# V by Strassen products kept in DRAM, q scaled during K's projection, and the softmax moved by one turn, in an attention and mixture-of-experts block

## The chip, the core and the metric

The kernel runs on one core of a Trainium2 chip, with all data in fp32. The time is what one execution takes on the device, in microseconds (us); the median of several executions is given. A profile is one execution recorded by the hardware. In it PE is TensorE's matmuls, PEld its weight loads, DVE VectorE, ACT ScalarE, POOL GpSimd, and SP the engine that issues the DMAs. An fp32 matmul leaves two records on PE.

## The reference, cut to what matters

```python
# x: (2, 512, 512); Wq, Wk, Wv: (512, 4096); Wo: (4096, 512); 32 heads of 128
h = layernorm(x)
q, k, v = h @ Wq + bq, h @ Wk + bk, h @ Wv + bv
q, k = rms_norm(q, gq), rms_norm(k, gk)             # over all 4096 columns
attn = softmax(einsum('bhqd,bhkd->bhqk', q, k) / sqrt(128))
x = x + layernorm(einsum('bhqk,bhkd->bhqd', attn, v) @ Wo + bo)
f = layernorm(x)
x = x + layernorm(f @ W_base.T + b_base + moe(f))   # 8 experts of rank 16, gated
```

## The kernel before

There are two batches of 512 tokens, 32 heads of 128 columns, and eight groups of four heads (a group is 512 columns of a weight). Heads and batches together make N = 64 pairs (head, batch), and the main loop goes over these 64 turns, head by head, both batches of a head one after the other.

**Norm and transposition.** `norm_transposed` (L132) normalizes the four token tiles of a batch and transposes them on PE. `xTs` holds the result for both batches: four tiles of 128 x 512 each, with the columns of `h` on the partitions.

**Projections of q and k.** `project` (L173) computes them transposed, one group of four heads at a time, by a Strassen scheme with seven products for eight blocks. The blocks are the two halves of the contraction, the two batches, and the two halves of a group's columns. `token_sums` (L150) makes the sums of tokens once. `weight_sums` (L162) makes the four sums of weights of each group on POOL, for the next group while PE works on this one. Each of the seven products is made for two head columns `j`, with two matmuls each (L192), and leaves PSUM by a DVE addition (L223 to L251) or, for the first, by an ACT activation that also adds the bias (L219). So a group has 28 matmuls on PE and 14 DVE operations. A finished head is stored in DRAM (`keptq`, `keptk`, L206), squared on ACT (L212) and added up on POOL (L213) for the RMS norm. Its tiles come from a pool of five buffers, `qpool` for q and `kpool` for k.

**Scales.** After K's first group the reciprocal root of q's mean square is made for all tokens (`rqs`, L284 to L286). After all of K, `key_scales` (L288) makes that of k.

**The head loop** (L434 to L455) does all else of the attention. One turn `i` issues:

- `fetch(i + 3)` (L315): loads k and q of that pair from DRAM; `scaled(i + 2)` (L323): multiplies q by its norm and by gq times gk, on DVE
- `sums(i)` (L345): three DVE additions over the four key tiles of the exponentials
- `scores(i + 1)` (L329): four matmuls (`pss`, L335), each leaving PSUM by ACT with k's scale (L336), then three DVE maxima (L338 to L340) and an all-reduce over the partitions on POOL (L342)
- `outward` (L398): products of an earlier group's outputs with Wo (`psy`, L404), dealt by the table `o_tasks`
- `values` (L304): V of a coming group, four matmuls for each token tile (`psv`, L308), leaving PSUM by an ACT copy (L310), dealt by `v_tasks`; V stays in SBUF, in 16 buffers
- `turned(i)` (L354): a DVE transposition and a reduction; `exponentials(i + 1)` (L374): a DVE subtraction of the maximum over 128 x 2048 (L376) and the exponential on ACT (L377)
- the additions of `outward` on DVE (L405)
- `weighted(i)` (L381): four matmuls of exponentials and V (`o`, L386); `reciprocals(i)` (L362): a small matmul (`psd`, L365), a reciprocal and a transposition on DVE; `divided(i)` (L389): a multiplication on DVE and the bias on ACT

**What sets the order.** PE, DVE, ACT and POOL run their instructions in the order of the code (`manual_schedule`, L575). SP's order is set by the framework: a DMA is queued when a planner holds its buffer and its data to be ready, and SP then takes its queue in order. PSUM has eight banks in two tags of four, `ps` and `aux`; `pt` (L68) takes them in turn if no tag is named.

**After the loop** the last group's outward products, the residual, a second norm and the mixture of experts (`ffn`, L501) follow.

Of the kernel before, what the change touches and what calls it, by code (L numbers as in the profile page):

```python
# [10 lines left out]
F32 = mybir.dt.float32  # L11
AF = mybir.ActivationFunctionType
ALU = mybir.AluOpType
# [18 lines left out]
def kernel(ctx: ExitStack, tc: tile.TileContext, x, wq, wk, wv, wo, vecs, rows, wbase, gates, bexp, out):  # L32
# [8 lines left out]

    nc = tc.nc
# [6 lines left out]
    vpool = ctx.enter_context(tc.tile_pool(name="vpool", bufs=2 * B * NT))  # L49
    qpool = ctx.enter_context(tc.tile_pool(name="qpool", bufs=5))  # L50
    kpool = ctx.enter_context(tc.tile_pool(name="kpool", bufs=5))
    opool = ctx.enter_context(tc.tile_pool(name="opool", bufs=GH * B + 10))
    spool = ctx.enter_context(tc.tile_pool(name="spool", bufs=3))
    tmp = ctx.enter_context(tc.tile_pool(name="tmp", bufs=6))
    wpool = ctx.enter_context(tc.tile_pool(name="wpool", bufs=4))
# [48 lines left out]
    gate_sb = const.tile([P, NK, E * R + E + 1], F32, tag="gate", name="gate_sb")  # L104
    nc.sync.dma_start(out=gate_sb, in_=gates.rearrange("(c p) f -> p c f", p=P))
    bexp_sb = const.tile([P, D], F32, tag="bexp", name="bexp_sb")
    nc.sync.dma_start(out=bexp_sb, in_=bexp)
# [42 lines left out]
    def token_sums(xTs):  # L150

        (b11, b21), (b12, b22) = ((xT[0:2], xT[2:4]) for xT in xTs)
        first, second = wide("t12"), wide("t34")
        t1, t2, t3, t4 = first[:, 0:2], first[:, 2:4], second[:, 0:2], second[:, 2:4]
        for c in range(2):
            nc.vector.tensor_tensor(t1[:, c], b12[c], b11[c], ALU.subtract)
            nc.vector.tensor_tensor(t2[:, c], b22[c], t1[:, c], ALU.subtract)  # L157
            nc.vector.tensor_tensor(t3[:, c], b22[c], b12[c], ALU.subtract)
            nc.vector.tensor_tensor(t4[:, c], b21[c], t2[:, c], ALU.subtract)
        return [[t[:, c] for c in range(2)] for t in (t1, t2, t3, t4)]  # L160
# [12 lines left out]
    def project(xTs, sums, w_src, bias, step, name, pool, keep, accs, w):  # L173
# [8 lines left out]
        parts = weight_sums(w, f"{name}0")  # L182
        for g in range(G):
# [20 lines left out]
            def keep_it(o, b, j):  # L204
                h = g * GH + j
                nc.sync.dma_start(out=keep[b, h], in_=o)  # L206
# [3 lines left out]
                else:  # L210
                    sq = tt(f"sq_{name}{b}_{h}")
                    nc.scalar.activation(sq, o, AF.Square)  # L212
                    nc.gpsimd.tensor_tensor(accs[b], accs[b], sq, ALU.add)  # L213

# [13 lines left out]
            t1, t2, t3, t4 = sums  # L228
            u2 = [tile_of("u2", j) for j in two]
            for j in two:  # L230
                ps = product(6, s2, t2, j)
                nc.vector.tensor_tensor(u2[j], ps, u1[j], ALU.add)
            u3 = [tile_of("u3", j) for j in two]
            for j in two:
                ps = product(7, s3, t3, j)
                nc.vector.scalar_tensor_tensor(u3[j], ps, column(step, j), u2[j], ALU.add, ALU.add)
            for j in two:
# [3 lines left out]
                keep_it(o, 0, j + 2)  # L241
            for j in two:
# [4 lines left out]
                keep_it(o, 1, j + 2)  # L247
            for j in two:
# [6 lines left out]
    def attention():  # L255
# [9 lines left out]
        rqs = [const.tile([P, 512], F32, tag=f"rq{b}", name=f"rq{b}") for b in range(B)]  # L265
# [3 lines left out]
        accq = [xpool.tile([P, 512], F32, tag="x", name=f"accq{b}") for b in range(B)]  # L269
        acck = [xpool.tile([P, 512], F32, tag="x", name=f"acck{b}") for b in range(B)]  # L270

        steps = const.tile([P, 2, H], F32, tag="steps", name="steps")
        for i in range(2):
            of, to = (v.rearrange("p (g j) -> p g j", j=GH) for v in (vec[:, i, :], steps[:, i, :]))
            nc.vector.tensor_tensor(to[:, :, 0:2], of[:, :, 2:4], of[:, :, 0:2], ALU.subtract)
        sums4 = []
        for _ in project(xTs, sums4, wq, bq, steps[:, 0, :], "q", qpool, keptq, accq, wq0):
            pass
        wk0 = load_w(wk[:, ts(0, GH * P)], "w_k0")
        for g in project(xTs, sums4, wk, bk, steps[:, 1, :], "k", kpool, keptk, acck, wk0):  # L280
            if g == 0:
                for b in range(B):
# [3 lines left out]
                    nc.vector.reciprocal(rqs[b], rqs[b])  # L286

# [7 lines left out]
        vs, wvs, wos = {}, {}, {}  # L295

        def load_wv(g):
            if g < H // GH:
# [314 lines left out]
```

## Time and profile before

| what | value |
|---|---|
| median of 3 runs | 1385.29 us (1385.04 to 1387.31) |
| the profiled execution | 1385.63 us, of which its span (first to last instruction) is 1383.9 |
| granted TensorE clock, mean | 0.991 |
| busy DVE, ACT, POOL | 907.3, 503.7, 351.0 us |
| DMA, whole span | 109.84 MB, mean 79 GB/s |
| stages in the span | start to 37 us; q to 224; k to 418; head loop to 1287; rest to 1384 |
| issue to landing, 256 KB: store of q, of k; load of q, of k | 2.5, 2.4; 2.9, 2.6 us (medians) |

A row of the profile by lines gives line, engine, operation, tiles out<-in, shapes and count, then busy time and the mean of one in ns, and the idle time before with what ended it. A row of the timeline gives start, duration, and the same names. In a table of windows each row is a stretch of time with the busy time of each engine and its instructions in brackets, then the granted clock, the busy share of the 16 DMA engines, and GB/s.

### The profile page before, as it was taken

How to read it: one execution, taken by the hardware profiler on the slowest of the kernel's cores; microseconds unless marked ns; L12 is line 12 of the kernel's file. 1: busy time of each engine (PE TensorE's matmuls, PEld its weight loads, DVE VectorE, ACT ScalarE, POOL GpSimd, SP SyncE). 2: the span in 40 equal slices, each digit the busy share in tenths (PEclk: the TensorE clock that was granted, in tenths of full speed). 3: DMA queues.
4: the chain of work that ended last, by engine and by line, in shares of the span. 5: the costliest groups of instructions: out<-in, count | busy, mean ns of one | idle time of the engine just before them, and what ended most of it. 6: DMA issues, size and time to landing. Idle time of an engine off the chain costs nothing.

```text
span 1383.9 us, 10495 instructions
## 1 busy us (share of the span) xinstructions
PE 1342.4 (97%) x3308; PEld 610.3 (44%) x3308; DVE 907.3 (66%) x1350; ACT 503.7 (36%) x703; POOL 351.0 (25%) x262
## 2 busy tenths in 40 slices
PE   4999999999999999999999999999999999999976
PEld 2444444444444444444444444444444444444443
DVE  6443434534343888778778777777777777887556
ACT  4122222322224444344434344343434343443333
POOL 3357556565731111111111111111111111111000
PEclk9999999999999999999999999999999999999998
DMA  6243344434333112103112111211111111200001
GB/s 231 91 150 124 117 149 144 161 106 152 122 118 118 61 46 76 46 31 107 40 37 76 61 46 61 67 40 64 58 61 42 65 48 59 76 23 16 23 1 61
DMA packets 58759, 109.84 MB, mean 79 GB/s; under 512 B 5072, under 2 KB 5712, under 8 KB 58704
## 3 DMA queue, kind: packets, MB, share of 16 engines
q1 hardware_dynamic: 58704, 109.17, 23.2%
q8 instruction: 26, 0.43, 0.1%
q14 instruction: 29, 0.24, 0.1%
HBM read 73.50 MB, written 35.65 MB: 79 GB/s over the span
## 4 chain that ended last, share of the span: by engine, by line
PE 95%; DVE 3%; ACT 1%; issue 1%; POOL 0%; DVEq 0%; POOLq 0%; ACTq 0%
PE pss L335 16%; PE psy L404 16%; PE o L386 16%; PE psv L308 15%; PE p_k L192 14%; PE p_q L192 14%; PE f L517 2%; PE f L567 1%; PE psd L365 1%; PE hg L509 1%; DVE same L264 0%; PE nt_f L139 0%; PE nt_a L139 0%; DVE nT_a L144 0%; ACT n_a L137 0%
## 5 line engine op out<-in xcount | busy, mean ns | idle before, releaser
L342 POOL PARTITION_ALL_REDUCE top<-m x64 | 114.1, 1783 | 738.7 <-DVE m L340 738.7
L335 PE MATMUL pss<-qh,kh 128*128 128x512 f32 x512 | 235.2, 602 | 0.0
L386 PE MATMUL o<-s,v 128*128 128x512 f32 x512 | 230.2, 592 | 0.0
L308 PE MATMUL psv<-wv,nT_a 128*128 128x512 f32 x512 | 229.5, 592 | 0.0
L404 PE MATMUL psy<-wo,oh 128*128 128x512 f32 x512 | 228.2, 592 | 0.0
L376 DVE TENSOR_TENSOR s<-s,top 128x2048 f32<-128x2048 f32 x64 | 146.7, 2292 | 42.5 <-POOL top L342 42.5
L377 ACT ACTIVATE s<-s 128x2048 f32<-128x2048 f32 x64 | 122.2, 1910 | 89.4 <-DVE s L376 88.4
L336 ACT ACTIVATE s<-pss,rk 128x512 f32<-128x512 f32 x256 | 154.0, 680 | 0.8 <-PE pss L335 0.8
L386 PEld LDWEIGHTS o<-s,v 128*128 128x128 f32 x512 | 97.3, 190 | 122.5 <-issue 122.2
L308 PEld LDWEIGHTS psv<-wv,nT_a 128*128 128x128 f32 x512 | 97.1, 190 | 121.5 <-issue 121.0
L404 PEld LDWEIGHTS psy<-wo,oh 128*128 128x128 f32 x512 | 97.1, 190 | 121.5 <-issue 121.0
L310 ACT COPY v<-psv 128x512 f32<-128x512 f32 x64 | 37.4, 586 | 275.8 <-PE psv L308 275.8
L335 PEld LDWEIGHTS pss<-qh,kh 128*128 128x128 f32 x512 | 92.5, 190 | 92.8 <-issue 92.8
L213 POOL TENSOR_TENSOR accq<-accq,sq_q 128x512 f32<-128x512 f32 x62 | 78.6, 1268 | 95.0 <-ACT sq_q L212 94.5
L393 ACT ACTIVATE oh<-oh,vec 128x512 f32<-128x512 f32 x64 | 46.0, 719 | 144.0 <-DVE oh L392 144.0
L213 POOL TENSOR_TENSOR acck<-acck,sq_k 128x512 f32<-128x512 f32 x62 | 78.6, 1267 | 75.4 <-ACT sq_k L212 75.0
L367 DVE RECIPROCAL inv<-psd 128x16 f32<-128x16 f32 x64 | 16.4, 256 | 118.4 <-PE psd L365 118.4
L192 PE MATMUL p_q<-t,s_q 128*128 128x512 f32 x192 | 88.0, 608 | 3.6 <-DVE t L157 3.6
L212 ACT ACTIVATE sq_q<-q 128x512 f32<-128x512 f32 x62 | 39.1, 630 | 134.3 <-DVE q L240 79.2
L212 ACT ACTIVATE sq_k<-k 128x512 f32<-128x512 f32 x62 | 39.1, 631 | 127.9 <-DVE k L240 71.4
L192 PE MATMUL p_k<-t,s_k 128*128 128x512 f32 x192 | 85.0, 592 | 0.0
L192 PEld LDWEIGHTS p_q<-t,s_q 128*128 128x128 f32 x192 | 37.3, 195 | 51.3 <-issue 48.8
(146 smaller groups left out, 1440.2 us busy)
## 6 DMA issues: line engine op xcount, KB each, us to landing
keptq<-q SPq DMA_DIRECT2D x64, 256.0 KB, 2.5
qh<-keptq SPq DMA_DIRECT2D x64, 256.0 KB, 2.9
keptk<-k SPq DMA_DIRECT2D x64, 256.0 KB, 2.4
kh<-keptk SPq DMA_DIRECT2D x64, 256.0 KB, 2.6
w_q<-in_wq SPq DMA_DIRECT2D x8, 1024.0 KB, 6.9
w_k<-in_wk SPq DMA_DIRECT2D x8, 1024.0 KB, 5.6
wv<-in_wv SPq DMA_DIRECT2D x8, 1024.0 KB, 5.6
wo<-in_wo SPq DMA_DIRECT2D x8, 1024.0 KB, 5.0
```

What stands on the lines that cost most here:

```text
L192: nc.tensor.matmul(ps, a[:, c, ts(j, P)], x[c], start=(c == 0), stop=(c == 1))
L212: nc.scalar.activation(sq, o, AF.Square)
L213: nc.gpsimd.tensor_tensor(accs[b], accs[b], sq, ALU.add)
L308: nc.tensor.matmul(ps, xTs[b][c][:, ts(t, P)], wvs[g][:, c, :], start=(c == 0), stop=(c == NK - 1))
L335: nc.tensor.matmul(ps, kk[i][:, ts(k, P)], qs[i], start=True, stop=True)
L336: nc.scalar.activation(s[:, k, :], ps, AF.Copy, scale=rks[b][:, k : k + 1])
L342: nc.gpsimd.partition_all_reduce(top, m, P, ReduceOp.max)
L376: nc.vector.tensor_tensor(s, s, top.unsqueeze(1).to_broadcast([P, NT, 512]), ALU.subtract)
L377: nc.scalar.activation(s, s, AF.Exp)
L386: nc.tensor.matmul(po, vs[b, g, k][:, ts(j, P)], ss[i][:, k, :], start=(k == 0), stop=(k == NT - 1))
L393: nc.scalar.activation(o, o, AF.Identity, bias=bv[:, h : h + 1], scale=1.0)
L404: nc.tensor.matmul(ps, o[:, ts(t, P)], wos[g][:, j, :], start=(j == 0), stop=(j == GH - 1))
```

## The change

**V.** `values` now uses the same seven products, with the roles turned: the blocks are the two halves of the contraction, the two batches, and the two groups of a pair of groups. Its result has tokens on the partitions. For each of the four pairs of groups, `values` goes twice through the seven products (for token tiles 0 and 1, then 2 and 3), and each product takes two matmuls. One step is one product of one token tile: 28 steps for a pair. The weight tile of a product (two 128 x 512 tiles) is loaded two products ahead into one of three buffers. The sums of weights come from DRAM (`keptw`): `value_sums` makes them on POOL, one call after each group of Q's projection. Product 1 leaves PSUM by an ACT copy, products 2, 6, 7, 4 and 3 by a DVE addition, product 5 by two. Finished V tiles are stored in DRAM (`keptv`), and `fetch_v` loads a group's eight tiles in the last two turns of the group before. The first pair's 28 steps run ahead of the head loop, the second pair's over turns 0 to 7, the last 56 over turns 8 to 43.

**q.** `scaled` moves into K's projection: from the second group on, `between` is called five times per group and each time loads, scales and stores two tiles of q (`keptqs`), which the head loop then loads.

**The softmax.** A turn now starts with `sums` and `turned` of the turn before, then subtracts (`below_top`), then issues the next scores, the exponential, and the division of the turn before. The maxima are a part of their own, `top_of`, ahead of the PSUM additions of V and of `outward`. Each turn from the ninth on has one outward product of the group before; scores and `psd` use tag `ps`, V, `outward` and `weighted` use tag `aux`.

**Buffers.** `wpool` has two buffers and not four; the token sums lie in `xpool`, the outputs `ys` in a pool of their own; the gates and `bexp` are loaded after the head loop.

The diff, cut to its core:

```diff
+    ypool = ctx.enter_context(tc.tile_pool(name="ypool", bufs=B * NT))
+    upool = ctx.enter_context(tc.tile_pool(name="upool", bufs=7))
+    vpool = ctx.enter_context(tc.tile_pool(name="vpool", bufs=3 * NT))
...
+    wpool = ctx.enter_context(tc.tile_pool(name="wpool", bufs=2))
+    hpool = ctx.enter_context(tc.tile_pool(name="hpool", bufs=3))
...
             t1, t2, t3, t4 = sums
+            between()
             u2 = [tile_of("u2", j) for j in two]
...
+        def value_sums(p, c):
+            a11, a12, a21, a22 = ws = [kpool.tile([P, 512], F32, tag="k", name=f"a{i}_v{p}_{c}") for i in range(4)]
+            for w, (q, k) in zip(ws, ((0, 0), (0, 1), (1, 0), (1, 1))):
+                nc.sync.dma_start(out=w, in_=wvq[k, c, :, 2 * p + q, :])
+            s1, s3, s4 = a22, a21, a12
+            s2 = kpool.tile([P, 512], F32, tag="k", name=f"s2_v{p}_{c}")
+            nc.gpsimd.tensor_tensor(s1, a21, a22, ALU.add)
+            nc.gpsimd.tensor_tensor(s2, s1, a11, ALU.subtract)
+            nc.gpsimd.tensor_tensor(s3, a11, a21, ALU.subtract)
+            nc.gpsimd.tensor_tensor(s4, a12, s2, ALU.subtract)
+            for i, w in enumerate((s1, s2, s3, s4)):
+                nc.sync.dma_start(out=keptw[p, i, c], in_=w)
...
+        def scaled(i):
+            h, b = divmod(i, B)
+            q = qpool.tile([P, 512], F32, tag="q", name=f"qr{b}_{h}")
+            nc.sync.dma_start(out=q, in_=keptq[b, h])
+            nc.vector.scalar_tensor_tensor(q, q, gqk[:, h : h + 1], rqs[b], ALU.mult, ALU.mult)
+            nc.sync.dma_start(out=keptqs[b, h], in_=q)
...
+        for g in project(xTs, sums4, wq, bq, steps[:, 0, :], "q", qpool, keptq, accq, weight_sums(wq0, "q0")):
+            if g == NG - 2:
+                k_parts = weight_sums(load_w(wk[:, ts(0, GH * P)], "w_k0"), "k0")
+            value_sums(g // 2, g % 2)
+        for g in project(xTs, sums4, wk, bk, steps[:, 1, :], "k", kpool, keptk, acck, k_parts, between=scale_some):
             if g == 0:
...
+                pending.extend(range(N))
...
-            v = vpool.tile([P, 512], F32, tag="v", name=f"v{b}_{g}_{t}")
-            nc.scalar.copy(v, ps)
-            vs[b, g, t] = v
...
+            order = ((1, b11), (2, b21), (6, t2), (7, t3), (4, t4), (5, t1), (3, b22))
+            todo = [(p, tiles, i, x) for p in range(NG // 2) for tiles in ((0, 1), (2, 3)) for i, x in order]
...
+                for t in tiles:
+                    ps = pt(f"v{i}_{p}_{t}", "aux")
+                    for c in range(2):
+                        nc.tensor.matmul(ps, x[c][:, ts(t, P)], w[:, c, :], start=(c == 0), stop=(c == 1))
...
+                        def keep(b, half, u):
+                            o = tile_of(f"o{b}{half}")
+                            nc.vector.tensor_tensor(o, ps, u, ALU.add)
+                            nc.sync.dma_start(out=keptv[b, 2 * p + half, t], in_=o)
...
+        def fetch_v(b, g):
+            for t in range(NT):
+                v = vpool.tile([P, 512], F32, tag="v", name=f"v{b}_{g}_{t}")
+                nc.sync.dma_start(out=v, in_=keptv[b, g, t])
+                vs[b, g, t] = v
...
         for i in range(N):
             g, n = divmod(i, G)
             if i + 3 < N:
                 fetch(i + 3)
-            if i + 2 < N:
-                scaled(i + 2)
-            if n == 4:
+            if n == 2:
                 load_wo(g)
-                load_wv(g + 2)
-            d = sums(i)
+            if n >= G - 2 and g + 1 < NG:
+                fetch_v(n - G + 2, g + 1)
+            part = turned(i - 1, sums(i - 1)) if i > 0 else None
+            below_top(i)
             if i + 1 < N:
                 scores(i + 1)
-            adds = [outward(*task) for task in o_tasks[i]]
-            for task in v_tasks[i]:
-                values(*task)
-            part = turned(i, d)
-            if i + 1 < N:
-                exponentials(i + 1)
-            for add in adds:
-                add()
+            exponentials(i)
+            if i > 0:
+                divided(i - 1, po, reciprocals(i - 1, part))
+            exits = []
+            want = 28 * (i + 1) // G if i < G else 28 + 56 * (i + 1 - G) // (5 * G - 4)
+            while left and 84 - left < want:
+                exits.append(next(v_steps))
+                left -= 1
+            adds = [outward(g - 1, n)] if g > 0 else []
+            top_of(i + 1)
+            for work in exits + adds:
+                work()
             po = weighted(i)
-            divided(i, po, reciprocals(i, part))
+        divided(N - 1, po, reciprocals(N - 1, turned(N - 1, sums(N - 1))))
```

## The prediction

> **What bounds the kernel now.** I read the engines' busy time first, then the chain of work that ended last, then the windows by stage, then the timeline of one turn of the head loop.
>
> ```profile
> PE 1342.4 (97%) x3308; PEld 610.3 (44%) x3308; DVE 907.3 (66%) x1350; ACT 503.7 (36%) x703; POOL 351.0 (25%) x262
> ...
> PE 95%; DVE 3%; ACT 1%; issue 1%; POOL 0%; DVEq 0%; POOLq 0%; ACTq 0%
> PE pss L335 16%; PE psy L404 16%; PE o L386 16%; PE psv L308 15%; PE p_k L192 14%; PE p_q L192 14%; PE f L517 2%; PE f L567 1%; PE psd L365 1%; PE hg L509 1%; DVE same L264 0%; PE nt_f L139 0%; PE nt_a L139 0%; DVE nT_a L144 0%; ACT n_a L137 0%
> ```
>
> TensorE carries 95% of the chain, and V's products (psv, L308) are 15% of it. A matmul less is time less, as long as nothing else becomes late. Windows: K's projection, the start of the head loop, its middle. The first number is the length, then PE, PEld, DVE, ACT, POOL, clock, DMA share, GB/s:
>
> ```profile
> 224.00:418.00 194.00, 194.00 (x454) 85.90 (x453) 83.22 (x114) 52.47 (x82) 117.94 (x95) 1.00 0.40 137
> 418.00:466.00 48.00, 46.96 (x126) 21.74 (x124) 26.23 (x32) 19.20 (x28) 7.86 (x5) 1.00 0.27 86
> 533.00:1200.00 667.00, 667.00 (x1629) 301.50 (x1628) 514.16 (x686) 271.43 (x344) 88.84 (x50) 1.00 0.17 58
> ```
>
> PE never rests there; DVE is 77% busy in the loop, 43% in K's projection, where POOL has 61%. One turn, on PE:
>
> ```profile
> 699.85 0.29 PE L365 MATMUL psd<-part,same 128*128 128x16 f32 x2
> 699.99 3.68 PE L335 MATMUL pss<-qh,kh 128*128 128x512 f32 x8
> 703.51 3.60 PE L404 MATMUL psy<-wo,oh 128*128 128x512 f32 x8
> 706.94 3.60 PE L308 MATMUL psv<-wv,nT_a 128*128 128x512 f32 x8
> 710.38 3.60 PE L386 MATMUL o<-s,v 128*128 128x512 f32 x8
> 713.81 0.29 PE L365 MATMUL psd<-part,same 128*128 128x16 f32 x2
> ```
>
> A turn is 13.96 us: four tasks of eight records, each 3.43 us from start to start (703.51 to 706.94), so a record costs 0.429 us and an fp32 matmul (two records) 0.859; psd adds some 0.2.
>
> **The change, part by part.** The sum is made against the profiled execution: 1385.63 us, of which 1383.9 is the span. The median of the runs shown, 1385.29, is 0.3 lower, which is nothing here.
>
> *V's products.* Now 64 tiles of 4 matmuls: 256. Then 4 pairs of groups, 4 token tiles, 7 products, 2 matmuls: 224. 32 fewer at 0.859 us: **-27.5 us**, all on the path.
>
> *V's exits on DVE.* 64 ACT copies (586 ns, L310) become 16. For each of 16 pairs of pair and token tile DVE gets seven additions (one each for products 2, 6, 7, 4 and 3, two for 5) of 0.69 us (L232, L251): 112, of them 28 ahead of the loop and 84 (58 us) in it. The 64 scalings (L325, 48.8 us) leave the loop for K's projection. A turn of DVE without scaling, from start to start in the timeline (d 0.72, 0.72, 0.75; dT 0.74; part 0.61; s 2.21; inv 0.29; r 0.75; o 0.61; m 0.79, 0.80, 0.61; y 0.62), is 10.2 us. PE per turn: 10.5 without V (3 x 3.43 + 0.2). The diff deals V as 28 steps of 1.72 us over turns 0 to 7 (no outward product there), 56 over turns 8 to 43, none over 44 to 63:
>
> - turns 0-7: PE 7.1 + 3.5 x 1.72 = 13.1, DVE 9.6 + 3.5 x 0.65 = 11.9
> - turns 8-43: PE 10.5 + 1.56 x 1.72 = 13.2, DVE 10.2 + 1.0 = 11.2
> - turns 44-63: PE 10.5, DVE 10.2
>
> So PE hides DVE everywhere, in the last 20 turns with 0.3 us only; what DVE needs beyond that there is paid 20 times.
>
> *The softmax a turn later.* Now inv waits for psd (118.4 us in 52 waits) and s for the all-reduce (42.5). After the change sums and turned of i-1 open the turn while PE does scores(i+1) (3.43 us), the 2.29 us subtraction covers psd, and the additions, sums and turned cover the 1.78 us all-reduce. PE's weighted(i) needs the exponential, which ends some 6 us into the turn, and starts at 9.7 or (late turns) 7.1. I cost this at nothing. The PE pause of 1.04 us in the first turn (46.96 of 48) should go: **-1.0**. At the end nothing hides the last turn: without scores, PE waits for part (about 1.1), for the exponential (0.7) and for part of turn 63 (0.2): **+2.0** (0 to 6).
>
> *V through DRAM.* Stores (16.8 MB), reloads (16.8), seven weight tiles twice a pair (29.4 for 8.4 now), and the sums of weights on POOL during Q's projection (8 calls of 4 x 1.27 = 41 us; POOL has 104 busy of 187 there, and the stores of its sums stand among those of q on SP, whose five buffers cover a short wait). In the loop that makes some 110 GB/s, against over 300 shown below. Three output tiles of the seven in the pool are free, and bursts of additions can wait for a store (0.32 issue, 2.4 landing): I take **+1** (0 to 6).
>
> *Scaling q during K's projection.* This is the disputed part. From group 1 on, each of five places in a K group loads, scales and stores two q tiles: 10 per group of 28 matmuls, 24.05 us, thus one per 2.4 us. Behind a waiting scaling on DVE stand the additions of products that free PSUM; eight banks let PE run ahead by about six tiles, 10 us, before it stops. Bytes per group: 8 stores and a weight tile (3.15 MB) plus 20 transfers of 262 KB (5.24): 8.39 MB, 349 GB/s. The DMA at its densest, first q reloads between K's stores, then a weight tile, then reloads of k:
>
> ```profile
> 226.00:228.00 2.00, 2.00 (x6) 0.95 (x5) 0.00 (x0) 0.97 (x2) 2.00 (x2) 1.00 0.93 299
> 228.00:230.00 2.00, 2.00 (x6) 0.88 (x5) 0.69 (x1) 0.19 (x1) 1.92 (x3) 1.00 1.00 354
> 294.00:298.00 4.00, 4.00 (x10) 1.73 (x10) 2.06 (x5) 1.41 (x3) 2.75 (x3) 1.00 1.04 404
> 418.00:420.00 2.00, 2.00 (x7) 0.81 (x5) 1.89 (x3) 0.63 (x1) 1.55 (x2) 1.00 0.92 282
> ```
>
> At 282/0.92 = 307 GB/s a group takes 27.3 us (2.73 per scaling); at 354, 23.7. With five tiles loaded ahead, the other 59 scalings at 2.73 come 59 x 0.33 = 19 us late; less PE's 10 us, that is 9. At 340, the mean of 226 to 230 (those are q reloads, the nearest rows), the lateness is 4 and hidden. DVE loses more beside POOL, since a scaling reads two operands from SBUF:
>
> ```profile
> 12.56 1.27 POOL L167 TENSOR_TENSOR s_q<-w_q 128x512 f32<-128x512 f32 x1 [3.08 <-DMA w_q<-in_wq]
> 12.57 1.27 DVE L117 SCALAR_TENSOR_TENSOR shift_a<-mv_a,rs_a 128x1 f32<-128x1 f32 x1
> ...
> 418.72 2.77 DVE L325 SCALAR_TENSOR_TENSOR qh<-qh,gqk,rq 128x512 f32<-128x512 f32 x2
> ...
> 419.67 1.27 POOL L213 TENSOR_TENSOR acck<-acck,sq_k 128x512 f32<-128x512 f32 x1 [0.45 <-ACT sq_k L212]
> ```
>
> The 128x1 operation (0.16 us elsewhere) ended with POOL's; two scalings took 2.77 us for 1.48, the longest 1.79 for 0.741. If every scaling took 1.4 (half of that pair), DVE would have 10 x 1.4 + 14 x 0.65 = 23.1 us per group: still under 24.05. I take **+4**, midway between 0 and 9; the far end is rival 1.
>
> The Trainium skill, page "SBUF — State Buffer", section "Who interferes with whom", says that a DVE instruction with two SBUF inputs contends with a GpSimd instruction that reads SBUF, and that whoever is first holds the shared pair for the whole instruction. That speaks against this change twice: for the scalings, where the rows above agree, and for sums(i), which the change puts right behind the start of an all-reduce and which no row here shows beside one. By the rule the sum would be 1382.
>
> The page "DMA: Bandwidth & Descriptors", section "Specifications", puts HBM at about 358 GB/s per core. The trace went to 404 on a weight tile, so the measurement decides. By the page's figure K's group would take 23.4 us and the term would be 0.
>
> *Sum*: -27.5 - 1.0 + 2.0 + 1 + 4 = -21.5; 1385.6 - 21.5 = **1364 us**.
>
> **Rivals.**
>
> 1. *The round trip of the five q buffers binds K's projection.* For it: SP issues in order, and a reload must wait for the store out of its buffer. Landings reached 7.3 us on k's tensor and 5.8 on q's, against medians of 2.4 to 2.9. With these worst ones (0.32 + 5.8 + 0.38 + 7.3 + 1.79 = 15.6 us, over five: 3.1 per scaling) 59 x 0.71 = 42 late, less 10: 32 instead of my 4, **1392 us**, slower. The gain is gone from 3.0 us per scaling (59 x 0.6 - 10 = 25). Against it: q reloads landed in 4.1 at most, four in a row at 225 to 230.
> 2. *All-reduce against sums.* The all-reduce starts 0.86 us after the start of the last maximum (706.13, 706.99) and lasts 1.78; in turns 44 to 63 sums(i) would start 1.23 after it. Held until the end it is 1.41 late, less 0.19 (the held scaling ended 0.55 after POOL, not 0.74). DVE's turn is 11.4 instead of 10.2, PE's 10.5: 20 x 0.9 = 18, **1382 us**, about no change. Earlier turns hide it behind V. For it: the rows above. Against it: they show elementwise operations of POOL, no all-reduce; DVE's transposes beside one kept 0.70, but read one operand.
> 3. *It doesn't do what it says:* the program's order on SP is not the code's (the trace has weight tiles of later groups ahead of stores); if V's loads or stores stand behind waits for PE, the gain is paid back in stalls: half of it, **1375 us**.
>
> **How the numbers follow.** Forecast (1357 to 1370) 0.55; rival 1 at its far end 0.12; rival 2 0.15; rival 3 0.18 (a third of it slower than before). Best case: terms 0 except -28.5 gives 1357. The range is 1357 to 1388: rival 2 and two thirds of 3 are inside, the far end of rival 1 and the slow third of 3 outside (0.18). 0.2%, 2.8 us, is about what a measurement can tell from no change: faster, below 1382.5: 0.55, two thirds of rival 3 (0.12) and half of rival 2 (0.07), 0.74; same: the other half, 0.08; slower: 0.12 + 0.06 = 0.18.
>
> **What would show it.** 448 records of V at 0.43 us; PE without pauses in K's groups (24.05 us each), turns of 13.1, 13.2 and 10.5 us. Wrong: K's groups longer than 24.5 with DVE waiting for a q load; scalings near 1.8 us; sums well over 0.69 behind an all-reduce and late turns of 11.5; PE waiting for a v tile or a weight tile of V.

## The result, and the profile after

The changed kernel takes 1386.04 us (median of 12 runs, 1380.98 to 1393.14), the kernel before 1385.72 (12 runs, 1383.03 to 1387.31). The ratio is 1.0009, with a 95% interval of 0.9992 to 1.0026: no change. The forecast was 1364. The profiled execution took 1384.94 us, of which the span is 1382.9, and so stands for the median within 0.1%.

The page of the changed kernel: busy engines, then the chain of work that ended last by engine.

```profile
PE 1325.8 (96%) x3244; PEld 599.5 (43%) x3244; DVE 1005.3 (73%) x1462; ACT 489.6 (35%) x655; POOL 402.4 (29%) x294
...
PE 53%; DVE 15%; DMA 1%; issue 1%; ACT 0%; DVEq 0%; SPq 0%; ACTq 0%
```

PE has 64 records fewer (3308 before): the 32 matmuls are gone. But the chain that carried 95% of the span on PE now runs over PE for 53% and over DVE for 15%: somewhere DVE has become what PE waits for.

Where, the stages tell. Each is taken from PE's timeline; "K's groups 2 to 8" are the seven groups beside which q is scaled, and "V and head loop" runs from the first matmul of V to the last `psd`.

| stage, us | before | after | difference |
|---|---|---|---|
| start to K's projection | 223.9 | 223.4 | -0.5 |
| K's first group | 25.8 | 25.8 | 0 |
| K's groups 2 to 8 | 168.2 | 185.7 | **+17.5** |
| V and head loop | 868.6 | 851.1 | **-17.5** |
| rest | 97.4 | 97.0 | -0.4 |

So the change is no idle one: two effects of 17.5 us cancel. The windows of the changed kernel show both sides. First four groups of K, then two single turns of the loop (length, then PE, PEld, DVE, ACT, POOL with their instructions, granted clock, DMA share, GB/s):

```profile
249.10:273.10 24.00, 24.00 (x57) 10.64 (x56) 22.34 (x23) 6.23 (x10) 13.70 (x11) 1.00 0.57 198
297.20:321.20 24.00, 24.00 (x58) 10.60 (x56) 15.72 (x20) 4.87 (x8) 14.27 (x11) 1.00 0.87 295
321.20:349.60 28.40, 25.90 (x58) 11.21 (x57) 19.86 (x25) 6.10 (x10) 17.11 (x12) 0.94 0.85 291
380.40:410.00 29.60, 26.00 (x58) 11.18 (x57) 21.68 (x27) 6.10 (x10) 17.31 (x12) 0.94 0.85 297
```

```profile
643.00:657.00 14.00, 14.00 (x35) 6.32 (x35) 11.16 (x16) 5.16 (x6) 1.78 (x1) 1.00 0.24 76
1224.67:1235.37 10.70, 10.70 (x27) 4.70 (x26) 10.29 (x14) 5.27 (x7) 1.78 (x1) 1.00 0.08 25
```

The loop is as forecast: PE without a gap, and DVE just below it in a late turn (10.29 of 10.70). K's first three scaled groups take 24 us each, full; from 321 on, three groups take 28 to 31 each, of which PE works 26, and the last, with four scalings only, 24.9. The column to see is DVE's: in these rows it has 15.7 to 22.3 us of work in a group, less than the group lasts, and yet PE waits for it. PE's timeline there:

```profile
304.03 7.03 PE L192 MATMUL p_k<-t,s_k 128*128 128x512 f32 x16
...
330.73 8.72 PE L192 MATMUL p_k<-t,s_k 128*128 128x512 f32 x16 [2.50 <-DVE u_k L250]
...
365.06 5.19 PE L192 MATMUL p_k<-t,s_k 128*128 128x512 f32 x8 [3.30 <-DVE k L256]
...
391.02 8.80 PE L192 MATMUL p_k<-t,s_k 128*128 128x512 f32 x16 [3.60 <-DVE u_k L250]
```

In brackets stands the pause and what ended it: an addition that empties PSUM. The five pauses of this stage come to 11.5 us. Behind the three shown the matmuls are slower as well: 16 records take 8.72 where they take 7.03 undisturbed, and 8 take 5.19 for 3.60. That makes some 5 of the other 6.0 us of the 17.5. There the granted clock is at 0.50 for 3.4 us, hence the 0.94 in these windows; when that happens is worked out in the last section.

What DVE did at 365, from its own timeline:

```profile
358.47 0.67 DVE L250 TENSOR_TENSOR u_k<-p_k,u_k 128x512 f32<-128x512 f32 x1
359.07 0.91 DVE L307 SCALAR_TENSOR_TENSOR qr<-qr,gqk,rq 128x512 f32<-128x512 f32 x1
363.57 0.75 DVE L307 SCALAR_TENSOR_TENSOR qr<-qr,gqk,rq 128x512 f32<-128x512 f32 x1 [3.59 <-DMA qr<-keptq]
364.24 1.28 DVE L256 TENSOR_TENSOR k<-p_k,u_k 128x512 f32<-128x512 f32 x2
```

DVE stands still for 3.59 us before a scaling whose q has not landed, and the addition `k` (L256), ready long before, is queued behind it. PE starts again at 365.06, when that addition has emptied a bank. The groups by line say how much of this there is; behind the first bar busy time and mean ns, behind the second the idle time before:

```profile
L212 POOL TENSOR_TENSOR acck<-acck,sq_k 128x512 f32<-128x512 f32 x62 | 87.0, 1405 | 81.8 <-ACT sq_k L211 79.6
L192 PE MATMUL p_k<-t,s_k 128*128 128x512 f32 x192 | 90.5, 622 | 11.5 <-DVE u_k L250 7.6
L307 DVE SCALAR_TENSOR_TENSOR qr<-qr,gqk,rq 128x512 f32<-128x512 f32 x64 | 68.3, 1088 | 42.7 <-DMA qr<-keptq 37.4
L212 POOL TENSOR_TENSOR accq<-accq,sq_q 128x512 f32<-128x512 f32 x62 | 78.7, 1269 | 54.5 <-ACT sq_q L211 53.9
```

A scaling takes 1088 ns (741 undisturbed), POOL's sums of squares 1405 beside it against 1269 in Q's projection, and DVE waits 37.4 us for loads of q. Which of the two sinks PE, or both, the runs have to say.

### The profile page after: what moved, and what is told of

Its sections match the earlier page's. It is cut to its first block, busy times and chain, and to the rows that moved or that the text cites. A ratio compares the mean times of both kernels' runs of the same rounds, so it can differ in the third digit from the quotient of the medians.

```text
span 1382.9 us, 11315 instructions
## 1 busy us (share of the span) xinstructions
PE 1325.8 (96%) x3244; PEld 599.5 (43%) x3244; DVE 1005.3 (73%) x1462; ACT 489.6 (35%) x655; POOL 402.4 (29%) x294
## 4 chain that ended last, share of the span: by engine, by line
PE 53%; DVE 15%; DMA 1%; issue 1%; ACT 0%; DVEq 0%; SPq 0%; ACTq 0%
PE v L370 14%; PE pss L426 11%; PE psy L503 11%; PE o L485 11%; DVE s L473 3%; PE f L615 2%; DVE d L446 2%; DVE dT L454 1%; DVE d L448 1%; DVE d L447 1%; PE p_k L192 1%; DVE part L456 1%; DVE r L466 1%; DVE m L437 1%; DVE m L438 1%; DVE oh L491 1%
## 5 line engine op out<-in xcount | busy, mean ns | idle before, releaser
L427 ACT ACTIVATE s<-pss,rk 128x512 f32<-128x512 f32 x256 | 176.0, 687 | 458.4 <-PE pss L426 451.6
L426 PE MATMUL pss<-qh,kh 128*128 128x512 f32 x512 | 230.2, 592 | 0.0
L426 PEld LDWEIGHTS pss<-qh,kh 128*128 128x128 f32 x512 | 97.4, 190 | 122.7 <-issue 121.8
L370 PE MATMUL v<-w_v,t 128*128 128x512 f32 x256 | 118.3, 607 | 3.4 <-DMA w_v<-keptw 3.4
L212 POOL TENSOR_TENSOR acck<-acck,sq_k 128x512 f32<-128x512 f32 x62 | 87.0, 1405 | 81.8 <-ACT sq_k L211 79.6
L192 PE MATMUL p_k<-t,s_k 128*128 128x512 f32 x192 | 90.5, 622 | 11.5 <-DVE u_k L250 7.6
L307 DVE SCALAR_TENSOR_TENSOR qr<-qr,gqk,rq 128x512 f32<-128x512 f32 x64 | 68.3, 1088 | 42.7 <-DMA qr<-keptq 37.4
L212 POOL TENSOR_TENSOR accq<-accq,sq_q 128x512 f32<-128x512 f32 x62 | 78.7, 1269 | 54.5 <-ACT sq_q L211 53.9
L370 PE MATMUL v<-w_v,nT_a 128*128 128x512 f32 x192 | 88.3, 601 | 0.0
L504 DVE TENSOR_TENSOR y<-psy,y 128x512 f32<-128x512 f32 x56 | 38.3, 688 | 48.1 <-PE psy L503 48.1
L370 PEld LDWEIGHTS v<-w_v,t 128*128 128x128 f32 x256 | 47.1, 193 | 53.5 <-issue 53.0
L192 PEld LDWEIGHTS p_k<-t,s_k 128*128 128x128 f32 x192 | 38.0, 200 | 62.0 <-issue 60.2
```

What stands on the lines that cost most here:

```text
L192: nc.tensor.matmul(ps, a[:, c, ts(j, P)], x[c], start=(c == 0), stop=(c == 1))
L307: nc.vector.scalar_tensor_tensor(q, q, gqk[:, h : h + 1], rqs[b], ALU.mult, ALU.mult)
L370: nc.tensor.matmul(ps, x[c][:, ts(t, P)], w[:, c, :], start=(c == 0), stop=(c == 1))
L426: nc.tensor.matmul(ps, kk[i][:, ts(k, P)], qs[i], start=True, stop=True)
L427: nc.scalar.activation(s[:, k, :], ps, AF.Copy, scale=rks[b][:, k : k + 1])
```

## The experiments

Theory at first: the round trip of the five q buffers (load, scaling, store, load again), rival 1. Against it: the shared access of DVE and POOL, which makes each scaling longer; the bytes; the bursts of two scalings in a place. Where a time is that of one execution, the stages of that execution are compared and not the times.

**1 and 2. One half of the scaling alone.** In the first kernel the operation is left out and the load and the store stay; in the second the operation runs on resident tiles, and load and store are left out (the head loop then loads the unscaled q).

```diff
 # k_dma_only
             nc.sync.dma_start(out=q, in_=keptq[b, h])
-            nc.vector.scalar_tensor_tensor(q, q, gqk[:, h : h + 1], rqs[b], ALU.mult, ALU.mult)
             nc.sync.dma_start(out=keptqs[b, h], in_=q)
 # k_dve_only
-            nc.sync.dma_start(out=q, in_=keptq[b, h])
-            nc.vector.scalar_tensor_tensor(q, q, gqk[:, h : h + 1], rqs[b], ALU.mult, ALU.mult)
-            nc.sync.dma_start(out=keptqs[b, h], in_=q)
+            nc.vector.scalar_tensor_tensor(q, rqs[b], gqk[:, h : h + 1], rqs[1 - b], ALU.mult, ALU.mult)
```

> The scaling itself is left out: each q tile is loaded and stored again unscaled, so DVE never waits for a load in K's projection. In the changed kernel K's groups 2 to 8 take 185.7 us for 168.3 us of PE work, 17.4 too long. Theory D (DVE stands in its queue behind a late q load, so PSUM fills up): the 17.4 shrink to under 3, whatever the DMA carries. Theory P (DVE and POOL hold each other up at the scalings): under 3 too. Theory B (the traffic itself delays K's stores and weights): still over 10.

> The scalings stay as DVE instructions with two operands in SBUF, on resident tiles; the load and the store of q for each are left out, and the head loop reads the unscaled q. Theory D: groups 2 to 8 fall to 168 to 171 us, and the mean scaling stays near 1.09 us. Theory P: they stay at 180 or more. Theory B: 168 to 171.

One execution each: 1365.44 and 1364.34 us. K's groups 2 to 8 take 168.2 in both, as before the change. The transfers alone cost nothing, with DMA moving 318 GB/s in this stage against 284 in the changed kernel, so the bytes are no limit. The contention alone costs nothing either: the scalings are even slower here, on average 1255 ns.

```profile
L306 DVE SCALAR_TENSOR_TENSOR qr<-rq,gqk,rq 128x512 f32<-128x512 f32 x64 | 77.9, 1255 | 0.0
```

**3. Twelve buffers.** The complete function; every second scaling takes its tile from the pool of the token sums (`upool`), which is idle during K's projection.

```diff
-            q = qpool.tile([P, 512], F32, tag="q", name=f"qr{b}_{h}")
+            pool, tag = ((qpool, "q"), (upool, "u"))[i % 2]
+            q = pool.tile([P, 512], F32, tag=tag, name=f"qr{b}_{h}")
```

> Full function; the scaled tiles come from qpool and upool in turn, so 12 buffers and not five. Theory D in the form of my first rival (the round trip of five buffers): the 17.4 us shrink to under 5 and the time falls by 12 or more, to about 1372. If the bytes are the limit (about 8.4 MB per group at 290 GB/s, 29 us): groups stay at 28 or more and the time within 4 us of the changed kernel. Theory P: no change.

1368.36 us (4 runs, 1364.90 to 1372.84), a ratio to the kernel before of 0.9883 (0.9859 to 0.9906): faster than both kernels. K's groups take 168.2. Groups by line:

```profile
L212 POOL TENSOR_TENSOR acck<-acck,sq_k 128x512 f32<-128x512 f32 x62 | 88.4, 1426 | 60.7 <-ACT sq_k L211 58.9
L308 DVE SCALAR_TENSOR_TENSOR qr<-qr,gqk,rq 128x512 f32<-128x512 f32 x64 | 75.8, 1220 | 4.5 <-DMA qr<-keptq 4.5
```

The waits fall from 37.4 to 4.5 us while each scaling gets longer (1220): with a reserve of loaded tiles DVE can afford the contention.

**4. An operation with one operand** from SBUF, a transposition, in the scaling's place; so q is transposed and not scaled.

```diff
-            nc.vector.scalar_tensor_tensor(q, q, gqk[:, h : h + 1], rqs[b], ALU.mult, ALU.mult)
+            nc.vector.transpose(q, q)
```

> The scaling is replaced by a DVE transposition of the same tile, which has one operand in SBUF and takes 0.71 us beside an all-reduce as well as alone; so the values are not scaled, and loads and stores stay. Theory P: mean 0.71 instead of 1.09, POOL's additions back from 1.41 to 1.27, and the 17.4 us shrink to under 5. Theory D: the operation gets shorter, but the waits for q loads stay near 37 us and the 17.4 stay over 10.

One execution, 1373.70 us; K's groups 175.3, between the two.

```profile
L212 POOL TENSOR_TENSOR acck<-acck,sq_k 128x512 f32<-128x512 f32 x62 | 78.6, 1270 | 85.9 <-ACT sq_k L211 83.6
...
L307 DVE STREAM_TRANSPOSE qr<-qr 128x512 f32<-128x512 f32 x64 | 43.6, 698 | 58.1 <-DMA qr<-keptq 52.9 <-issue 4.7
```

POOL is back at 1270 and the operation at 698 ns, so the contention comes with the two-operand operation; it lengthened both sides. The waits on loads grow to 52.9, but the 4 us per group that DVE saves on ten operations pay for more than half of the loss. Contention and waits add up.

**5. The scaling of q alone, in the kernel before**, with its five buffers.

```diff
+        def scaled(i):
+            q = qpool.tile([P, 512], F32, tag="q", name=f"qr{b}_{h}")
+            nc.sync.dma_start(out=q, in_=keptq[b, h])
+            nc.vector.scalar_tensor_tensor(q, q, gqk[:, h : h + 1], rqs[b], ALU.mult, ALU.mult)
+            nc.sync.dma_start(out=keptqs[b, h], in_=q)
...
-            if i + 2 < N:
-                scaled(i + 2)
```

> Full function: the kernel before with one part of the change alone, q scaled and stored during K's projection, five buffers. Theory D: K's groups 2 to 8 get as long as in the changed kernel (168.2 to about 185) and the head loop gains nothing, since PE was never late there: about 1402 us. If the stretch came from V's part of the change (weight sums in DRAM, two weight buffers): K stays at 168 and the time at 1386.

One execution, 1399.41 us: K's groups 182.0 (+13.8), V and the loop 868.6 as before. The loss needs nothing of V's part.

**6. All of the change but the scaling**, which goes back into the loop.

```diff
-            q = qpool.tile([P, 512], F32, tag="q", name=f"qr{b}_{h}")
-            nc.sync.dma_start(out=q, in_=keptq[b, h])
-            nc.vector.scalar_tensor_tensor(q, q, gqk[:, h : h + 1], rqs[b], ALU.mult, ALU.mult)
-            nc.sync.dma_start(out=keptqs[b, h], in_=q)
+            nc.vector.scalar_tensor_tensor(qs[i], qs[i], gqk[:, h : h + 1], rqs[b], ALU.mult, ALU.mult)
...
+            if i + 2 < N:
+                scaled(i + 2)
```

> Full function: the changed kernel with only the scaling of q undone, back in the head loop two turns ahead on DVE (the pool of head outputs has 12 buffers instead of 13, to make room). K's groups 2 to 8 back at 168.2 us. If DVE is the bound of turns 44 to 63 (10.70 us there, where PE needs 10.52), each of them grows by the 0.66 of a scaling, to 11.36, so V and the loop take 848 + 13 = 861 us and the kernel about 1377. If DVE had room there, 848 and 1364.

One execution, 1373.74 us: K's groups 168.2, V and the loop 858.0 (-10.6 against before). A late turn is 11.3 us, bound by DVE. One late turn's DVE; the all-reduce runs from 1181.84 to 1183.62:

```profile
1182.19 1.23 DVE L304 SCALAR_TENSOR_TENSOR qh<-qh,gqk,rq 128x512 f32<-128x512 f32 x1
1183.35 0.68 DVE L440 TENSOR_TENSOR d<-s 128x512 f32<-128x512 f32 x1
1184.06 0.69 DVE L441 TENSOR_TENSOR d<-d,s 128x512 f32<-128x512 f32 x1
```

The scaling now stands first behind the start of the all-reduce and takes 1.23, and the first addition is back at 0.68. Taking the scaling out of the loop is worth some 10 us there, if K's projection has room for it.

**7. The sums by one reduction**, on top of the twelve buffers.

```diff
-            nc.vector.tensor_tensor(d, s[:, 0, :], s[:, 1, :], ALU.add)
-            nc.vector.tensor_tensor(d, d, s[:, 2, :], ALU.add)
-            nc.vector.tensor_tensor(d, d, s[:, 3, :], ALU.add)
+            nc.vector.tensor_reduce(d, s.rearrange("p k f -> p f k"), AX.X, ALU.add)
```

> Full function, on the kernel with 12 buffers: the three additions of sums become one DVE reduction over the four key tiles, which has one operand in SBUF. If the first addition is long (1.24 for 0.68 us in late turns) because it meets the all-reduce, the reduction does not meet it: some 2.1 us from start to end for 2.75, turns 44 to 63 fall from 10.70 to 10.52, 3.6 us less in all than 12 buffers alone (1368.4), about 1365. If a reduction over a stride costs more than the additions, late turns get longer than 10.7 and the time goes up.

1395.9 us (4 runs, 1390.26 to 1399.18), ratio to before 1.0085 (1.0059 to 1.0111). My price for the operation was wrong:

```profile
L447 DVE TENSOR_REDUCE d<-s 128x512 f32<-128x2048 f32 x64 | 236.2, 3691 | 0.0
```

3691 ns, against 2.2 us for the three additions. It bears only on the question of rival 2, which experiment 6 and the timeline below answer without it.

**8. The scalings spread** over seven places of a group instead of five, of two and one, with five buffers.

```diff
-            for _ in range(2):
+            places[0] += 1
+            for _ in range(1 + (places[0] % 7 in (1, 3, 5))):
```

> Full function, five buffers: the ten scalings of a K group are spread over all seven products (2, 1, 2, 1, 2, 1, 1) instead of two ahead of each of five. If the bursts are what five buffers can't feed (two per 3.43 us), DVE's waits for q loads fall from 37 us to under 15 and K's stretch from 17.4 to under 6. If the mean round trip is what counts, both stay within a third of what they were.

One execution, 1381.25 us; K's groups 182.5 instead of 185.7. DVE's idle time ahead of the scalings stays (43.0 us for 42.7), and so do PE's pauses (11.2 us for 11.5); what is gone is the half clock behind them. So the bursts are not the cause. At this point I put it down to the mean round trip: 11.5 us of pauses behind some 10 us of lag, over 59 scalings, made 2.76 us per scaling, 13.8 for a round of five. That gives a number for each other count of buffers, and the next two runs test it.

**9 and 10. Six and seven buffers**: every sixth scaling, or two of seven, take the idle pool.

```diff
 # k_6_buffers
+            pool, tag = ((qpool, "q"), (upool, "u"))[i % 6 == 5]
 # k_7_buffers
+            pool, tag = ((qpool, "q"), (upool, "u"))[i % 7 in (3, 6)]
```

> The changed kernel, but every sixth scaling of q takes its tile from the idle pool of the token sums, so that the other five of six rotate in the five buffers as before: six buffers in effect. Theory, the mean round trip binds: K's groups 2 to 8 took 185.7 with five buffers, 11.5 of it in PE pauses after some 10 us of lag that PSUM covers, so the 59 scalings were some 21.5 late, 0.36 each, 2.76 per scaling or 13.8 for a round of five. With six a scaling comes every 2.3 us, under the 2.4 that a group allows: K's groups 168 to 170, about 1365 in all. Rival, single long landings bind and only a deep reserve covers them: a sixth buffer takes off little, K's groups 178 to 184, 1376 or more.

> The same with two of seven scalings in the idle pool: seven buffers in effect, a round of 13.8 us gives 1.97 per scaling. Theory, the mean round trip binds: K's groups 168.2, without pauses, 1364. Rival, single long landings bind: 172 to 180, 1370 to 1378, still well over the 168.2 of twelve buffers.

One execution each, 1386.97 and 1377.08 us; K's groups 182.6 and 172.8, DVE still waiting 31.6 and 23.7 us for transfers. **The theory fell**: a mean of 2.3 or 1.97 us per scaling would have left no wait. Both stages lie in the ranges of the rival, single long landings. (V and the loop took 855 and 856 us in these two, with a late tile of V, see below; so their times are longer than the stage of K alone would make them.) Seven buffers have few waits, but long ones. SP's issue of a weight tile of K up to the reloads behind it, and the waits on DVE after three such tiles:

```profile
376.19 0.40 SPq L86 DMA_DIRECT2D w_k<-in_wk  x1
376.96 0.32 SPq L213 DMA_DIRECT2D keptk<-k  x1
378.39 1.99 SPq L309 DMA_DIRECT2D keptqs<-qr  x2
380.66 1.08 SPq L213 DMA_DIRECT2D keptk<-k  x2
381.80 0.96 SPq L307 DMA_DIRECT2D qr<-keptq  x2
384.54 0.32 SPq L213 DMA_DIRECT2D keptk<-k  x1
385.13 0.94 SPq L307 DMA_DIRECT2D qr<-keptq  x2
```

```profile
335.33 2.83 DVE L308 SCALAR_TENSOR_TENSOR qr<-qr,gqk,rq 128x512 f32<-128x512 f32 x2 [6.23 <-DMA qr<-keptq]
362.52 2.92 DVE L308 SCALAR_TENSOR_TENSOR qr<-qr,gqk,rq 128x512 f32<-128x512 f32 x2 [5.94 <-DMA qr<-keptq]
388.39 3.49 DVE L308 SCALAR_TENSOR_TENSOR qr<-qr,gqk,rq 128x512 f32<-128x512 f32 x2 [4.53 <-DMA qr<-keptq]
```

The waits ended 26 to 27 us apart, about a group, and each 12.2 to 12.5 us after the issue of a weight tile (322.88, 350.11, 376.19). Between a tile's issue at 376.19 and the next reload of q lie 5.6 us, in which SP issues five stores.

**11 and 12. One weight tile for all of K**, with seven and with five buffers: six loads of 1 MB are left out, and groups 2 to 8 use the weights of the first.

```diff
-                w = load_w(w_src[:, ts(g + 1, GH * P)], f"w_{name}{g + 1}")
+                w = kw[0] if name == "k" else load_w(w_src[:, ts(g + 1, GH * P)], f"w_{name}{g + 1}")
```

> The kernel with seven buffers, and all groups of K use the weights of the first group, so that six of K's loads of 1 MB are left out; the sums of weights are made as before. The mean round trip has fallen as the whole cause: with six and seven buffers DVE still waited 31.6 and 23.7 us for loads. With seven, five of the six waits come 11.8 to 13 us after the issue of a weight tile. Theory, the tile delays the reloads behind it: without it the waits on loads of q fall under 8 us and K's groups 2 to 8 go from 172.8 to 168.2. Rival, the reloads are late because of SP's order, where they stand behind stores that wait for DVE: the waits stay at 15 or more, K's groups 171 to 174.

> The changed kernel with its five buffers and the same one weight tile for all of K. There are about three waits per group, one of which follows the tile. Theory, both the short round trip and the tile: the waits on loads of q fall from 37.4 to 20 to 28, K's groups 2 to 8 from 185.7 to 172 to 180. Rival, the tile alone: 168.2. Second rival, the round trip or SP's order alone: 183 to 187.

One execution each: 1365.69 and 1374.30 us. Seven buffers first, then five:

```profile
L310 DVE SCALAR_TENSOR_TENSOR qr<-qr,gqk,rq 128x512 f32<-128x512 f32 x64 | 77.7, 1252 | 0.0
```

```profile
L309 DVE SCALAR_TENSOR_TENSOR qr<-qr,gqk,rq 128x512 f32<-128x512 f32 x64 | 74.5, 1189 | 22.0 <-DMA qr<-keptq 21.9
```

With seven buffers and no weight tiles every wait is gone, and K's groups take 168.2. With five, 21.9 us of short waits remain (2.9 at most), and K's groups take 169.9, less than the 172 to 180 expected. So there are two sources of waits: the buffers' round trip and the weight tile; the second kernel lies nearer to the 168.2 of the rival than to the range of the theory.

How the tile acts, the two kernels with five buffers tell. In them the tile of one scaling is that of the fifth after it: in both traces no reload is issued before the store of five scalings earlier has landed, and the quickest comes 0.016 us behind. So a round can be taken apart, from the start of a scaling to the start of the fifth after it (means of 59 rounds, in us):

| part of a round | five (after) | five, one weight tile |
|---|---|---|
| the scaling | 1.10 | 1.21 |
| its end to the issue of its store | 0.10 | 0.22 |
| the store, issue to landing | 3.32 | 3.29 |
| that landing to the issue of the reload | **4.07** | **1.60** |
| the reload, issue to landing | 3.83 | 3.80 |
| that landing to the next scaling | 1.54 | 2.50 |
| sum | 13.96 | 12.62 |

On the mean the tile doesn't make the transfers longer (reloads issued up to 8 us behind one took 4.2 to 6.0 us, about 1 us more); what it changes is when SP issues the reloads. Ahead of the eleven waits of over 1.5 us in the changed kernel, the landings took 3.1 and 3.8 us, and the free buffer stood for 7.0 us before its reload was issued. What SP itself waited for in this stage of the changed kernel, in us, times, and the longest:

```profile
SPq L308 <- DVE qr L307: 64.2, 53, 3.6
```

L308 is the store of a scaled tile. SP takes its queue in order, so a reload behind such a store waits for a scaling on DVE, while DVE waits for the reload. Without the tile SP waits less for scalings (37.1 us), and more for stores of q to land, ahead of reloads (5.7 us become 32.6): the reloads come to the head of its queue sooner. Why they do, with one DMA of 1 MB per group less (8.39 MB become 7.34), is not shown; SP's order is the planner's.

**What the runs say together.** DVE's time per group is 14 additions (14 x 0.66 = 9.2 us), ten scalings, and ten times the idle time before a scaling; the columns come from each kernel's groups by line (idle time divided by 64, times ten). PE's floor is 24.0.

| kernel | additions | scalings | waits | sum | group measured |
|---|---|---|---|---|---|
| twelve buffers | 9.2 | 12.2 | 0.7 | 22.1 | 24.0 |
| scaling without transfers | 9.2 | 12.6 | 0 | 21.8 | 24.0 |
| seven, one weight tile | 9.2 | 12.5 | 0 | 21.7 | 24.0 |
| five, one weight tile | 9.2 | 11.9 | 3.4 | 24.5 | 24.3 |
| seven | 9.2 | 11.5 | 3.7 | 24.4 | 24.7 |
| five, one operand | 9.2 | 7.0 | 9.1 | 25.3 | 25.0 |
| seven places, five | 9.2 | 9.9 | 6.7 | 25.8 | 26.1 |
| six | 9.2 | 11.8 | 4.9 | 25.9 | 26.1 |
| the scaling alone in the kernel before, five | 9.2 | 11.6 | 5.4 | 26.2 | 26.0 |
| five (after) | 9.2 | 10.9 | 6.7 | 26.8 | 26.5 |

On the mean of the seven groups, a group lasts as long as the longer of PE's floor and this sum, within 0.3 us. That is bookkeeping, not a forecast: the waits had to be measured, and it does not hold group by group (in the changed kernel the second and third have some 28 us and last 24.0, since PE still runs ahead, and the last has four scalings only). But it names the bound. DVE's queue holds the additions that PE needs behind loads that come late, and without contention the same waits would cost less.

## Why the prediction was wrong

**V's products: right.** V and the loop went from 868.6 to 848.0 with twelve buffers (undisturbed K) and 851.1 in the changed kernel. The terms for this part (-27.5 - 1.0 + 2.0 + 1) made -25.5, so 843.1. What the 4.9 us to 848.0 are made of:

- Late turns: 10.52 us at first, as said (10.5), then 10.70 for eleven turns: 2.0. This is rival 2, in small. A late turn of the changed kernel:

```profile
1101.95 1.78 POOL L440 PARTITION_ALL_REDUCE top<-m  x1 [8.91 <-DVE m L438]
...
1102.30 1.24 DVE L446 TENSOR_TENSOR d<-s 128x512 f32<-128x512 f32 x1
1103.57 0.69 DVE L447 TENSOR_TENSOR d<-d,s 128x512 f32<-128x512 f32 x1
```

The first addition of `sums` starts 0.35 behind the all-reduce and takes 1.24 instead of 0.69: it is held for 0.55 and ends at 1103.54, before the all-reduce does (1103.73). Rival 2 had the start right (1.23 - 0.86 = 0.37 behind) and had it held to the end. The Trainium skill, page "SBUF — State Buffer", section "Who interferes with whom", says that whoever issues first gets the shared pair for the whole instruction; it says so of DVE's two-port modes, and the prediction took it for two operands and an all-reduce too. That isn't what this row shows, as far as POOL's rough spans go: with the pair held to 1103.73 the addition could not have ended before. So DVE's turn became 10.7 and not 11.4.

- The end of the loop: PE waits 2.80, 0.28 and 0.33 us, 3.4 where I had 2.0.
- A weight tile of V that comes late in the part before the loop: 1.31 with twelve buffers, so near the 1 us set for V's way through DRAM. In the changed kernel it is 3.39, with slower matmuls after it, and with seven buffers 7.00:

```profile
440.86 13.21 PE L371 MATMUL v<-w_v,t 128*128 128x512 f32 x24 [7.00 <-DMA w_v<-keptw]
```

SP issued that tile at 435.01, behind loads of k (L414) that waited there for the last stores of K to land. That is rival 3, in one place.

About 1 us stays unplaced. PE had no gap in the loop's middle, and a pair of turns there takes 26.2 us, as forecast (13.2 for one).

**q during K's projection: the step that failed.** I took +4, midway between 0 and 9, and it measured +17.5. Some parts were right. A scaling was to take up to 1.4 us, it took 1.09. The bound of 340 to 354 GB/s held, since twelve buffers moved up to 352 in a group. Reloads were to be some 10 us late before PE feels it, and PE first paused at 328, in the fourth scaled group.

What failed is the pace of the scalings. The term took it from bytes per second (2.47 to 2.73 us each). But in the changed kernel a buffer goes round in 13.96 us, 2.79 per scaling, where PE's group leaves 2.4. Of these 13.96, 1.5 us are a loaded tile's own wait for DVE, and 4.1 are time in which the buffer is free and SP has not yet issued its reload. These 4.1 were put at nothing: they are in no term, and not in rival 1 either. In the kernel with one weight tile they are 1.6, and K's groups take 169.9 instead of 185.7.

With it failed the sentence "If every scaling took 1.4 (half of that pair), DVE would have 10 x 1.4 + 14 x 0.65 = 23.1 us per group: still under 24.05." It judged DVE's work against the group alone, and the lateness of the loads in another sentence, as though the two had separate slack. They stand in one queue: 20.1 us of work and 6.7 of waits make 26.8. With 23.1 the room for waits was 0.9 us a group; the price of ten waits of unknown length had to be put beside that. The weight tile was counted as bytes in the group's mean. Its bytes do fit, but with it the reloads are issued 2.5 us later on the mean. Last, 6.0 of the 17.5 us are PE time lost beside the pauses themselves, most of it at half clock, which no term had.

**Rival 1** named the place, the five buffers, and the chain in which PE waits for DVE and DVE for a load. Its price came from the worst landings (5.8 and 7.3 us in a round of 15.6, 3.1 per scaling). That this is near the 13.96 measured is luck: the landings were 3.8 and 3.3 us on the mean, and the 4.1 between them were not in it. With a term open from 0 to 32 us, a forecast that took 4 had less behind it than the 0.55 I gave.

**What stays open**: why SP's queue brings the reloads later when a weight tile is among its loads; and why executions of the changed kernel and of that with twelve buffers spread over 12 and 8 us, where those of the kernel before stay within 4.3. The three slowest of the changed kernel (1389.65 to 1393.14 us) have the lowest mean clocks, 0.981 to 0.984, so PE's pauses may differ from one execution to the next.

## What to carry to other kernels

Before work is put into an engine that has "room", add up in one queue its work, the stretching by contention, and the waits that come with the work's own loads; compare the sum with the period, not each part. A load, operation and store of a tile through DRAM needs buffers for the whole round, and that is more than the operation and the two transfers: here a free buffer waited 4.1 us on the mean, and up to 13.5, until a queue that serves its entries in order came to its reload. Five buffers lost all that the rest of the change had gained, twelve from a pool that was idle anyway kept it. And a total that doesn't move is read by stages first: here two terms of 17.5 us stood behind a ratio of 1.0009.

## What the runs showed of the hardware

- Whether PE is slower after a pause depends on where the pause falls. In the traces of this case the granted clock is 1.0 or 0.5 and changes only at points that lie whole multiples of 3.41 us apart. Two such stretches and the one behind each, first of the changed kernel, then of experiment 5 (columns as above: length, PE busy, and so on, the clock third from the end):

```profile
327.20:330.60 3.40, 1.03 (x3) 0.19 (x1) 1.97 (x4) 0.52 (x1) 0.00 (x0) 1.00 0.96 289
330.60:334.00 3.40, 3.27 (x4) 1.51 (x5) 3.40 (x4) 0.74 (x2) 2.87 (x2) 0.50 1.00 349
```

```profile
331.20:334.60 3.40, 1.40 (x4) 0.33 (x2) 0.47 (x1) 0.00 (x0) 0.73 (x1) 1.00 0.79 257
334.60:338.00 3.40, 2.38 (x6) 1.21 (x7) 2.07 (x4) 2.38 (x4) 1.58 (x2) 1.00 1.02 346
```

  The first pause, 2.50 us, lies nearly whole in one stretch, which leaves PE busy for 0.30 of it; the next stretch has half the clock, and 16 records take 8.72 us instead of 7.03. The second, 3.02 us, is longer but lies across two; PE is busy for 0.41 of the first, the clock stays, and 8 records take 3.67 instead of 3.60. Over all fourteen traces, the clock went from 1.0 to 0.5 behind 63 stretches, all with PE busy for 0.38 or less (PE's ends are modelled), and stayed at 1.0 behind all with 0.41 or more; none lay between. So a pause of 2.2 us (six buffers) cost 1.8 us on top, and four of 2.8 to 3.1 us (experiment 5) only 0.1 each.
- A reduction over four tiles that lie 2 KB apart (128x2048 to 128x512) took 3.69 us, where three additions of the same data take 2.2.
- A two-operand addition on DVE behind the start of an all-reduce on POOL (1.78 us) was held for 0.55 us; over all 64 turns this addition takes 845 ns on average, against 700 where the scaling stands in its place.
- Contention of two-operand scalings with POOL's additions lengthened both, 741 to 1088 up to 1255 ns and 1269 to 1405 up to 1446; one-operand transpositions (698) left POOL at 1270.
